# Feed-forward weights in two sets of buffers instead of one, and later due times for the fp4 weights and the softmax attention

## The chip, the cores and the metric

The kernel runs on one core of one Trainium2 chip. The metric is device time in microseconds (us) of one execution. One execution was also profiled; its trace gives every instruction's start and duration on the engines: TensorE (PE for matmuls, PEld for the loading of their stationary operand), VectorE (DVE), ScalarE (ACT), GpSimd (POOL), and the SyncE queue that issues the DMAs (SPq).

## The reference

Four blocks in a row, each added to its own input, on x of shape (8, 1024, 256), all in float32:

```python
x = x + _L0_attn_ref(_layernorm(x), ...)   # block 1: linear "flow" attention, then a GELU feed-forward
x = x + _L0_ffn_ref(_layernorm(x), ...)    # block 2: ReLU feed-forward
x = x + _L1_attn_ref(_layernorm(x), ...)   # block 3: softmax attention, one head of 256
x = x + _L1_ffn_ref(_layernorm(x), ...)    # block 4: gated feed-forward with fp4 weights
```

The parts that the change touches:

```python
# block 1, after its attention: W1 is (256, 1024), W2 is (1024, 256)
ffn = jax.nn.gelu(h @ W1 + b1, approximate=False) @ W2 + b2
return _layernorm(h + ffn, ln2_g, ln2_b)
# block 2: w1 is (256, 1024), w2 is (1024, 256)
h = jax.nn.relu(jnp.einsum('bsd,dw->bsw', x, w1) + b1)
return jnp.einsum('bsw,wd->bsd', h, w2) + b2
# block 3
scores = jnp.einsum('bqd,bkd->bqk', Q, K) / jnp.sqrt(jnp.float32(D_K))
return jnp.einsum('bqk,bkv->bqv', jax.nn.softmax(scores, axis=-1), V)
# block 4: every operand, the three weights too, is rounded to fp4 in blocks of 16 along its rows
xq = fp4_quant_dequant(x); wq = fp4_quant_dequant(w)
return jnp.einsum('bsk,nk->bsn', xq, wq)
h = jax.nn.silu(gate) * y
```

Blocks 1, 2 and 4 work on each row alone, but for the running sums along the sequence in block 1's attention; block 3 needs all 1024 rows of its sequence first.

## The kernel before

**Tiles and stages.** A chunk is 128 rows, a group is 4 chunks (512 rows), a sequence is 2 groups; there are 16 groups, p = 0 to 15. Block 1's attention (`linear_group`, `linear_span`, `linear_chunk`) runs group after group, since it carries running sums; much of it is VectorE work, and twice a group it sends a small packed tile to DRAM and reads it back spread over the partitions (`packed`, `spread`). Its result is turned into `hT`, half a group (256 rows) at a time.

**The feed-forwards** are in `dense()` (line 1300). For every group, for block 1's and block 2's weights, for each half group, there are NF = 8 steps f. A step is a first product (two matmuls, 128x256 each, `w[:, k*P:]` stationary, into a bank), an activation into a `hidden` tile on ScalarE, and, LAG = 2 steps later, a second product (`second()`, two matmuls with `hidden` stationary and `w[:, D:]` moving) that accumulates over f. In the profile each of these is four records of 128x256, in float32. So a group has 32 steps, the run 512.

**Weights.** They are read anew for every half group: `load_weights()` (line 1345) gives each step one buffer `w_ff` of [128, 512], W_FF = 5 of them in turn, and loads both halves of it together: 128 columns of W1 (two 128x128 pieces) and 128 rows of W2, 128 KB each. The buffer is held from the load until the second product of its step has been issued: the load of step n has the condition `n < W_FF + seconds[0]`, where `seconds[0]` counts second products.

**Block 4's weights** are rounded and transposed by `fp4_weights()` (line 673) in 18 pieces of at most 128x256: load into a `w_raw` tile (up to three ahead), the DVE steps of `fp4`, a square on ScalarE, two transposes on TensorE, two copies on ScalarE. The last piece sets `"fp4" in weights`, which `soft_chunk` waits for in its second half.

**Blocks 3 and 4** run in `soft_chunk(cc)` (line 1464), one for each of the 64 chunks, started by `softmax_and_fp4()` (line 1603) in order, when the whole sequence is ready (`q["normed"] == NCH`). At most 4 chunks are in work, 8 once block 1's attention is done.

**The order of the work** is made when the program is built. All parts are generators; each `yield` is a need: an engine, the tiles to wait for, banks, a condition `when`, and a due time `at`. `Plan.run` (line 290) keeps a modelled clock of each engine and of the DMA queue and takes, again and again, the need with the smallest key: the time TensorE would wait for it, then how far it is from ripe (a DMA counts as ripe 3.0 us after its buffer was last used), then other engines before TensorE, and last the due time `at`. Due times are in units of groups: block 1's attention of group p is due from p to p + 0.74, its feed-forwards from p + 1 to p + 2, the weights at p + 0.9 + n % 32 / 32. The order so found is fixed on each engine's queue and on SyncE's; on the chip an instruction that waits holds up what is behind it in its queue. Every instruction is issued through one helper, so nearly all have line 331 in the profile; they are told apart by their tiles.

Of the kernel before, what the change touches and what calls it, by code (L numbers as in the profile page):

```python
# [9 lines left out]
F32 = mybir.dt.float32  # L10
# [6 lines left out]
P = 128  # L17
D = 256
# [6 lines left out]
W_FF = 5  # L25
RES = 10
HALVES = 5
LAG = 2
# [34 lines left out]
class Plan:  # L63
# [191 lines left out]
    def pe(self, *tiles, **kw):  # L255
        return self.need("tensor", tiles, **kw)
# [7 lines left out]
    def dma(self, *tiles, **kw):  # L264
        return self.need("sync", tiles, **kw)
# [84 lines left out]
def block_stack_kernel(ctx: ExitStack, tc: tile.TileContext, a: dict, out: bass.AP):  # L350
# [20 lines left out]
    plan = Plan(tc, tc.nc)  # L371
    nc, pe, dve, act, dma = plan, plan.pe, plan.dve, plan.act, plan.dma
# [117 lines left out]
    late = set()  # L490
# [132 lines left out]
    def two(t):  # L623
        return t.rearrange("p (k t) -> p k t", k=2)
# [48 lines left out]
    def fp4_weights():  # L673
        pieces = []
        for name, dstT in (("L1_ffn_w_gate", wgT), ("L1_ffn_w_up", wuT)):
            for r0, rows in INTER_TILES:
                turns = [(dstT[:, k, r0 : r0 + rows], k * P, P) for k in range(2)]
                pieces.append((a[name][r0 : r0 + rows, :], turns))
        for n in range(2):
            for c0 in range(0, INTER, D):  # L680
                width = min(D, INTER - c0)
                turns = []
                for f0 in range(0, width, P):
                    rows = min(P, width - f0)
                    dst = wdT[:rows, (c0 + f0) // P, n * P : (n + 1) * P]
                    turns.append((dst, f0, rows))
                pieces.append((a["L1_ffn_w_down"][n * P : (n + 1) * P, c0 : c0 + width], turns))
        raws = {}
        for i, (src, turns) in enumerate(pieces):
            for j in range(i, min(i + 3, len(pieces))):  # L690
                if j not in raws:
                    ahead = pieces[j][0]
                    raws[j] = (yield from fresh(
                        "soft",
                        dma(at=1.5 + 1.6 * i / len(pieces), when=lambda: count["stage"] == 4),
                        "w_raw",
                    ))[
                        : ahead.shape[0], : ahead.shape[1]
                    ]
                    nc.sync.dma_start(out=raws[j], in_=ahead)  # L700
            rows, width = src.shape
            raw = raws.pop(i)
            at = 1.5 + 1.6 * i / len(pieces)
            yield dve(raw, at=at)
            yield from fp4(raw, width, rows)
            yield pe(raw, banks=1)
            bank = tr_bank()
            for k, (dst, c0, n) in enumerate(turns):
                nc.tensor.transpose(bank[:n, k, :rows], raw[:, c0 : c0 + n], ident[:rows, :rows])
            plan.drop(raw)  # L710
            yield act(bank)
            for k, (dst, c0, n) in enumerate(turns):
                nc.scalar.copy(dst, bank[:n, k, :rows])
        weights.add("fp4")
# [585 lines left out]
    def dense():  # L1300


        behind = []

        def second():
            p, b, half, f, hidden, w = behind.pop(0)
            acc = accs.get((p, b, half))
            yield pe(
                hidden, banks=0 if f else 1, when=None if f else lambda: count["acc"] < 2
            )  # L1310
            if f == 0:
                acc = accs[p, b, half] = mm_bank()
                plan.keep(acc)
                count["acc"] += 1

            for c in range(2):
                nc.tensor.matmul(
                    acc[:, c * D : (c + 1) * D],
                    lhsT=hidden[:, c * P : (c + 1) * P],
                    rhs=w[:, D:],  # L1320
                    start=f == 0 and c == 0,
                    stop=f == NF - 1,
                    skip_group_check=True,
                )
            plan.drop(hidden)
            seconds[0] += 1
            if f == NF - 1:
                if (b, half) == (1, 1):
                    count["dense"] += 1
                left = [2]  # L1330

                def taken():
                    left[0] -= 1
                    if not left[0]:
                        plan.let_go(acc)
                        count["acc"] -= 1

                for j in range(2):
                    norms = (norms_1, norms_2)[b]
                    plan.start(  # L1340
                        norms(p, 2 * half + j, acc[:, j * D : (j + 1) * D], taken),
                        p + 1 + (2 * b + half + 1) / 4,
                    )

        def load_weights():
            ws, n = [], 0
            for p in range(flows):
                for wa, wb in (("L0_attn_W1", "L0_attn_W2"), ("L0_ffn_w1", "L0_ffn_w2")):
                    for f in 2 * list(range(NF)):
                        yield dma(  # L1350
                            at=p + 0.9 + n % 32 / 32,
                            when=lambda: n < W_FF + seconds[0] and count["stage"] >= 2,
                            unused=ws[n - W_FF :][:1] if n >= W_FF else (),
                        )
                        w = big.tile([P, 2 * D], F32, tag="w_ff", name="w_ff", bufs=W_FF)
                        cols = slice(f * P, (f + 1) * P)
                        nc.sync.dma_start(
                            out=two(w[:, :D]), in_=a[wa][:, cols].rearrange("(k p) n -> p k n", p=P)
                        )
                        nc.sync.dma_start(out=w[:, D:], in_=a[wb][cols, :])  # L1360
                        ws.append(w)
                        loaded.append(w)
                        n += 1

        loaded, seconds = [], [0]
        plan.start(load_weights(), 0.9)
        accs = {}
        for p in range(flows):
            for b, (kind, ba, func) in enumerate((("hT", b1, AF.Gelu), ("nT", fb1, AF.Relu))):
                for half in range(2):  # L1370
                    n_turned = groups[p]["turned"]
                    while behind and n_turned.get((kind, half)) != 2:
                        yield from second()
                    for f in range(NF):
                        yield pe(
                            at=p + 1 + (16 * b + 8 * half + f) / 32,
                            when=lambda: n_turned.get((kind, half)) == 2 and loaded and "dense" in late,
                        )
                        inT = groups[p][kind][half]
                        w = loaded.pop(0)  # L1380
                        yield pe(inT, w, banks=1)
                        bank = mm_bank()[:, : 2 * P]
                        for k in range(2):
                            nc.tensor.matmul(
                                bank,
                                lhsT=w[:, k * P : (k + 1) * P],
                                rhs=inT[:, k, :],
                                start=k == 0,
                                stop=k == 1,
                            )  # L1390
                        count["stage"] = 4
                        hidden = yield from fresh("hidden", act(bank))
                        table(func)
                        nc.scalar.activation(hidden, bank, func, bias=ba[:, f : f + 1])
                        behind.append((p, b, half, f, hidden, w))
                        if f == NF - 1:
                            count["halves"] -= 1
                        if len(behind) > LAG:
                            yield from second()
        while behind:  # L1400
            yield from second()
# [62 lines left out]
    def soft_chunk(cc):  # L1464
# [1 line left out]
        g, i = divmod(c, G)  # L1466
        q = seqs[s]
        n2T, vt = q["n2T"], q["vt"]
        at = 3 + cc / 4
        yield pe(  # L1470
            banks=1,
            when=lambda: count["asked"] == cc
# [130 lines left out]
    def softmax_and_fp4():  # L1603
        for cc in range(B * NCH):
            q = seqs[cc // NCH]
            yield dve(
                at=3 + cc / 4,
                when=lambda: q["normed"] == NCH and cc - count["out"] < (8 if plan.spare else 4) and "softmax" in weights and "ends" in late,
            )
            plan.start(soft_chunk(cc), 3 + cc / 4)  # L1610

    for part in (linear_attention(), masks(), late_constants(), zeros(), load_weights_and_rows(), dense(), softmax_and_fp4(), fp4_weights(), softmax_weights()):
        plan.start(part, 0.0)
# [43 lines left out]
```

## Time and profile before

| | |
|---|---|
| median of 3 runs | 2680.63 us (2677.88 to 2684.55) |
| profiled execution, time | 2684.53 us |
| profiled execution, span from first to last instruction | 2682.8 us |
| mean granted TensorE clock | 0.988 |
| ACT busy | 1253.2 us (47%) |
| POOL busy | 585.4 us (22%) |
| mean DMA rate over the span | 79 GB/s |
| weight loads, `w_ff` | 1024 DMAs of 128 KB, median 0.46 us each on SPq |

Busy time is time in which at least one instruction of the engine runs; matmuls overlap, and the ends of their records are modelled. A clock of 0.83 in a stretch means that TensorE ran at 83% of its full speed in the mean of that stretch. The windows of the profile give the busy time of each engine in a stretch of the span; what is left of the stretch is idle time. The prediction shows the lines that it uses.

### The profile page before, as it was taken

How to read it: one execution, taken by the hardware profiler on the slowest of the kernel's cores; microseconds unless marked ns; L12 is line 12 of the kernel's file. 1: busy time of each engine (PE TensorE's matmuls, PEld its weight loads, DVE VectorE, ACT ScalarE, POOL GpSimd, SP SyncE). 2: the span in 40 equal slices, each digit the busy share in tenths (PEclk: the TensorE clock that was granted, in tenths of full speed). 3: DMA queues.
4: the chain of work that ended last, by engine and by line, in shares of the span. 5: the costliest groups of instructions: out<-in, count | busy, mean ns of one | idle time of the engine just before them, and what ended most of it. 6: DMA issues, size and time to landing. Idle time of an engine off the chain costs nothing.

```text
span 2682.8 us, 45525 instructions
## 1 busy us (share of the span) xinstructions
PE 2600.5 (97%) x16687; PEld 2020.7 (75%) x16687; DVE 1937.8 (72%) x4368; ACT 1253.2 (47%) x2600; POOL 585.4 (22%) x1101
## 2 busy tenths in 40 slices
PE   6999999999999999999999999999999999999997
PEld 4777777777777877777777777777777777787765
DVE  7788786776858768586776858668586777855565
ACT  3444445546454453544445454453545435445342
POOL 1332222131212213132221212213122221212000
PEclk8899999999999999999999999999999999999999
DMA  3334232322223232232323223132322313222000
GB/s 87 98 107 142 79 95 74 95 70 86 70 81 105 69 87 66 75 107 64 103 62 89 72 77 109 60 89 70 93 77 72 103 58 87 74 75 81 28 16 8
DMA packets 286814, 211.88 MB, mean 79 GB/s; under 512 B 24704, under 2 KB 275072, under 8 KB 286592
## 3 DMA queue, kind: packets, MB, share of 16 engines
q1 hardware_dynamic: 286592, 208.97, 26.7%
q8 instruction: 133, 2.18, 0.3%
q14 instruction: 89, 0.73, 0.1%
HBM read 188.17 MB, written 20.71 MB: 78 GB/s over the span
## 4 chain that ended last, share of the span: by engine, by line
PE 81%; DVE 12%; DMA 3%; ACT 2%; issue 1%; POOL 1%; SPq 0%; DVEq 0%; ACTq 0%; POOLq 0%
PE bank L331 81%; DVE hid L331 1%; DVE prod L331 1%; DMA spread<-packed 1%; DVE n L331 1%; ACT L331 1%; DVE ln_st L331 1%; DVE x_amax L331 1%; DVE div L331 1%; DVE res L331 1%; DVE u L331 1%; DMA packed<-scale 1%; DVE q L331 0%; DVE ln_mv L331 0%; POOL ln_rstd L331 0%
## 5 line engine op out<-in xcount | busy, mean ns | idle before, releaser
L331 PE MATMUL bank<-half,w_ff 128*128 128x256 f32 x2048 | 535.5, 384 | 15.1 <-DMA w_ff<-in_L_ffn_w_dram 7.7
L331 PE MATMUL bank<-w_ff,hidden 128*128 128x256 f32 x2048 | 532.9, 384 | 0.0
L331 POOL TENSOR_SCALAR ln_ve<-ln_mv 128x1 f32<-128x1 f32 x384 | 103.3, 269 | 1747.3 <-DVE ln_mv L331 1739.3
L331 PEld LDWEIGHTS bank<-half,w_ff 128*128 128x128 f32 x2048 | 379.8, 191 | 93.3 <-issue 24.8
L331 PEld LDWEIGHTS bank<-w_ff,hidden 128*128 128x128 f32 x2048 | 370.6, 191 | 88.5 <-issue 39.1
L331 ACT ACT_TABLE_LOAD x298 | 382.3, 1283 | 5.2
L331 ACT ACTIVATE hidden<-bank,c_L_ffn_b 128x256 f32<-128x256 f32 x256 | 120.8, 472 | 298.9 <-PE bank L331 298.9
L331 POOL TENSOR_TENSOR ln_rstd<-ln_ve,neghalf 128x1 f32<-128x1 f32 x384 | 237.5, 619 | 32.0
L331 PE MATMUL bank<-n2T,qT 128*128 128x512 f32 x512 | 242.1, 596 | 1.1 <-ACT qT L331 1.1
L331 PE MATMUL bank<-vt,probT 128*128 128x256 f32 x1024 | 232.0, 380 | 0.0
L331 PEld LDWEIGHTS bank<-vt,probT 128*128 128x128 f32 x1024 | 193.3, 190 | 32.9 <-issue 2.9
L331 ACT ACTIVATE hidden<-bank,c_L_attn_b 128x256 f32<-128x256 f32 x256 | 119.7, 468 | 193.6 <-PE bank L331 192.9
L331 DVE TENSOR_TENSOR hid<-hid,bank 128x352 f32<-128x352 f32 x118 | 60.9, 516 | 199.0 <-PE bank L331 165.4
L331 PE MATMUL bank<-wdT,hqT 128*128 128x256 f32 x768 | 177.8, 381 | 0.8 <-ACT hqT L331 0.8
L331 PE MATMUL bank<-wgT,xqT 128*128 128x352 f32 x512 | 174.9, 464 | 0.6 <-ACT xqT L331 0.5
L331 PE MATMUL bank<-wuT,xqT 128*128 128x352 f32 x512 | 172.4, 459 | 0.0
L331 DVE TENSOR_TENSOR sc<-bank,triu 128x512 f32<-128x512 f32 x256 | 160.6, 679 | 13.0 <-PE bank L331 12.0
L331 PEld LDWEIGHTS bank<-wdT,hqT 128*128 128x128 f32 x768 | 144.5, 191 | 22.9 <-issue 1.7
L331 PEld LDWEIGHTS bank<-n2T,qT 128*128 128x128 f32 x512 | 94.3, 191 | 71.7 <-issue 61.3
L331 PEld LDWEIGHTS bank<-wuT,xqT 128*128 128x128 f32 x512 | 97.5, 190 | 54.5 <-issue 0.5
L331 PEld LDWEIGHTS bank<-wgT,xqT 128*128 128x128 f32 x512 | 95.2, 191 | 36.8 <-issue 1.9
L331 PE MATMUL bank<-ident,n 128*128 128x128 f32 x512 | 93.7, 278 | 21.8 <-DVE n L331 14.5
(213 smaller groups left out, 4363.8 us busy)
## 6 DMA issues: line engine op xcount, KB each, us to landing
w_ff<-in_L_attn_W_dram SPq DMA_DIRECT2D x512, 128.0 KB
w_ff<-in_L_ffn_w_dram SPq DMA_DIRECT2D x512, 128.0 KB
spread<-packed SPq DMA_DIRECT2D x90, 256.0 KB
x<-in_L_attn_inputs_dram SPq DMA_DIRECT2D x64, 128.0 KB
xr<-in_L_attn_inputs_dram SPq DMA_DIRECT2D x64, 128.0 KB
rows<-res SPq DMA_DIRECT2D x64, 128.0 KB
out_dram<-y SPq DMA_DIRECT2D x64, 128.0 KB
rows<-rows SPq DMA_DIRECT2D x56, 128.0 KB
```

The lines of the kernel that those rows point to most:

```text
L331: ins = method(*args, **kw)
```

## The change

The first-product and the second-product weights get buffers of their own, `w_in` and `w_out`, five of [128, 256] each: the same bytes as five of [128, 512]. `load_weights` is started twice, once for each. A `w_in` buffer is taken again after the first product and the activation of its step (`firsts`), a `w_out` buffer after the second product (`seconds`). The `w_out` loads are due LAG steps later. `second()` no longer carries its weight tile along: it waits until a `w_out` has been asked for, then for its landing. The fp4 weights are due from 2.5 to 4.0 instead of 1.5 to 3.1, and every chunk of blocks 3 and 4 is due half a unit later.

```diff
@@ fp4_weights
-                        dma(at=1.5 + 1.6 * i / len(pieces), when=lambda: count["stage"] == 4),
+                        dma(at=2.5 + 1.5 * i / len(pieces), when=lambda: count["stage"] == 4),
...
-            at = 1.5 + 1.6 * i / len(pieces)
+            at = 2.5 + 1.5 * i / len(pieces)
@@ dense
         def second():
-            p, b, half, f, hidden, w = behind.pop(0)
+            p, b, half, f, hidden = behind.pop(0)
             acc = accs.get((p, b, half))
-            yield pe(
-                hidden, banks=0 if f else 1, when=None if f else lambda: count["acc"] < 2
-            )
+            yield pe(when=lambda: w_out and (f > 0 or count["acc"] < 2))
+            w = w_out.pop(0)
+            yield pe(hidden, w, banks=0 if f else 1)
...
-                    rhs=w[:, D:],
+                    rhs=w,
...
-        def load_weights():
+        def load_weights(names, used, loaded, first):
             ws, n = [], 0
             for p in range(flows):
-                for wa, wb in (("L0_attn_W1", "L0_attn_W2"), ("L0_ffn_w1", "L0_ffn_w2")):
+                for name in names:
                     for f in 2 * list(range(NF)):
                         yield dma(
-                            at=p + 0.9 + n % 32 / 32,
-                            when=lambda: n < W_FF + seconds[0] and count["stage"] >= 2,
+                            at=p + 0.9 + (n % 32 + (0 if first else LAG)) / 32,
+                            when=lambda: n < W_FF + used[0] and count["stage"] >= 2,
                             unused=ws[n - W_FF :][:1] if n >= W_FF else (),
                         )
-                        w = big.tile([P, 2 * D], F32, tag="w_ff", name="w_ff", bufs=W_FF)
+                        tag = "w_in" if first else "w_out"
+                        w = big.tile([P, D], F32, tag=tag, name=tag, bufs=W_FF)
                         cols = slice(f * P, (f + 1) * P)
-                        nc.sync.dma_start(
-                            out=two(w[:, :D]), in_=a[wa][:, cols].rearrange("(k p) n -> p k n", p=P)
-                        )
-                        nc.sync.dma_start(out=w[:, D:], in_=a[wb][cols, :])
+                        if first:
+                            nc.sync.dma_start(
+                                out=two(w), in_=a[name][:, cols].rearrange("(k p) n -> p k n", p=P)
+                            )
+                        else:
+                            nc.sync.dma_start(out=w, in_=a[name][cols, :])
...
-        loaded, seconds = [], [0]
-        plan.start(load_weights(), 0.9)
+        firsts, seconds = [0], [0]
+        w_in, w_out = [], []
+        plan.start(load_weights(("L0_attn_W1", "L0_ffn_w1"), firsts, w_in, True), 0.9)
+        plan.start(load_weights(("L0_attn_W2", "L0_ffn_w2"), seconds, w_out, False), 0.9)
...
-                            when=lambda: n_turned.get((kind, half)) == 2 and loaded and "dense" in late,
+                            when=lambda: n_turned.get((kind, half)) == 2 and w_in and "dense" in late,
...
-                        w = loaded.pop(0)
+                        w = w_in.pop(0)
...
-                        behind.append((p, b, half, f, hidden, w))
+                        firsts[0] += 1
+                        behind.append((p, b, half, f, hidden))
@@ soft_chunk
-        at = 3 + cc / 4
+        at = 3.5 + cc / 4
@@ softmax_and_fp4
-                at=3 + cc / 4,
+                at=3.5 + cc / 4,
...
-            plan.start(soft_chunk(cc), 3 + cc / 4)
+            plan.start(soft_chunk(cc), 3.5 + cc / 4)
```

## The prediction

> **What bounds the kernel now.** First the page's engine line:
>
> ```profile
> span 2682.8 us, 45525 instructions
> PE 2600.5 (97%) x16687; PEld 2020.7 (75%) x16687; DVE 1937.8 (72%) x4368; ACT 1253.2 (47%) x2600; POOL 585.4 (22%) x1101
> ```
>
> TensorE bounds it. The change removes no matmul, so it can only win TensorE's idle time, 2682.8 - 2600.5 = 82.3 us, and what a lowered clock costs. Second, the windows by stage, to see where that time lies (columns: window, its length, busy time and instructions of PE, PEld, DVE, ACT, POOL, granted clock, DMA share, GB/s):
>
> ```profile
> 0.00:75.00 75.00, 48.60 (x350) 35.71 (x350) 56.14 (x144) 22.82 (x65) 15.72 (x41) 0.81 0.31 78
> 75.00:120.00 45.00, 45.00 (x363) 35.30 (x356) 30.66 (x65) 22.45 (x49) 14.86 (x29) 0.98 0.29 82
> 120.00:140.00 20.00, 15.94 (x62) 12.24 (x60) 17.71 (x33) 4.95 (x15) 5.21 (x9) 0.83 0.66 183
> ...
> 150.00:170.00 20.00, 16.27 (x110) 12.97 (x112) 14.17 (x41) 5.73 (x16) 3.72 (x10) 0.83 0.39 116
> ...
> 230.00:250.00 20.00, 16.14 (x87) 12.32 (x86) 17.07 (x37) 5.54 (x17) 4.28 (x8) 0.83 0.62 171
> ...
> 268.00:2500.00 2232.00, 2213.63 (x14375) 1728.48 (x14372) 1612.02 (x3605) 1081.31 (x2199) 503.93 (x933) 1.00 0.28 81
> 2500.00:2546.00 46.00, 43.74 (x200) 31.71 (x199) 26.93 (x69) 16.66 (x39) 2.95 (x8) 1.00 0.07 24
> 2546.00:2613.00 67.00, 63.32 (x277) 46.40 (x276) 46.10 (x103) 30.07 (x56) 2.25 (x6) 0.97 0.06 16
> 2613.00:2682.80 69.80, 51.24 (x203) 35.18 (x201) 40.78 (x89) 18.92 (x39) 2.21 (x6) 0.93 0.02 8
> ```
>
> I count the loss of a stretch as its length minus busy time times clock. Until 75 us the feed-forwards have not begun and the change reaches nothing. From 75 to 268 us three stretches lose 20 - 15.94 x 0.83 = 6.8, 20 - 16.27 x 0.83 = 6.5 and 20 - 16.14 x 0.83 = 6.6 us; the rest there some 2. The 2232 us of the middle idle 18.4 us, under 1%. The tail after 2500 us idles 182.8 - 158.3 = 24.5 us and loses 63.32 x 0.03 + 51.24 x 0.07 = 5.5 us of clock: 30 us. So about 70 us can be touched at all.
>
> Third, TensorE's waits up to 270 us and its timeline (start, length, what, idle before it and who ended it), to see what the change can remove of this:
>
> ```profile
> PE bank L331 <- DMA w_ff<-in_L_ffn_w_dram: 6.9, 2, 3.7
> 118.48 1.03 PE L331 MATMUL bank<-half,w_ff 128*128 128x256 f32 x4
> 129.67 2.07 PE L331 MATMUL bank<-half,w_ff 128*128 128x256 f32 x4 [3.75 <-DMA w_ff<-in_L_ffn_w_dram]
> 160.10 2.11 PE L331 MATMUL bank<-qz,k 32*128 32x256 f32 x16 [3.73 <-ACT qz L331]
> 237.22 2.07 PE L331 MATMUL bank<-half,w_ff 128*128 128x256 f32 x4 [3.11 <-DMA w_ff<-in_L_ffn_w_dram]
> ```
>
> Two of the three losses are waits for feed-forward weights; the third waits for block 1's attention. After each, four matmuls that take 1.03 us take 2.07.
>
> **Edit 1, separate buffers.** Removed: nothing; added: nothing. Still 1024 loads of 128 KB and 2048 + 2048 matmul records. What moves is when a buffer comes free. In a dense stretch a step lasts 1.73 us (the first products start at 114.17, 115.03 + 0.86, and so on: 8 records in 1.73 us). Before, the buffer of step n - 5 comes free after its second product, issued LAG = 2 steps late, and is needed by the first product of step n: some 2.5 steps, 4.3 us, for the wait, the queue and the landing. In the queue at the first stall the load was issued at 124.09 us, behind four loads of the attention, and the chain of waits shows it landing 5.54 us later:
>
> ```profile
> 121.44 2.55 SPq L331 DMA_DIRECT2D spread<-packed  x4
> 124.09 1.04 SPq L331 DMA_DIRECT2D w_ff<-in_L_ffn_w_dram  x2
> 124.09 5.54 DMA w_ff<-in_L_ffn_w_dram
> ```
>
> After, either kind has the five steps from its own use to its next, 8.65 us, 4.3 more than before. The two stalls idled 3.75 and 3.11 us, so both are covered. Gain: at most 6.8 + 6.6 = 13.4 us, at least 0, if TensorE merely meets the next wait earlier. I take 11: the 20 us stretches also hold waits for transposes of 0.65 and 0.75 us that stay, and the lead is only half a microsecond above the first stall.
>
> The Trainium skill, "TensorE: Matmul & The Clock Gate", section Part 1, has the clock fall to half only after an idle window of about 3.4 us; by that the 3.11 us wait would cost its own length alone, and this term would be nearer 9 than 11. The trace disagrees: after 3.11 us the four matmuls still took 2.07 us, and the clock of the stretch was 0.83; the measurement decides.
>
> Edit 1's costs: a pair of loads that had one need has two, so SyncE may stop at 512 more places. SPq issues take a median of 0.46 us, 1024 x 0.46 = 471 us of 2683, hidden under the matmuls; queued behind a load that waits are the `x`, `xr`, `rows`, `packed` and `spread` transfers. First-weight loads now wait for an earlier event, second-weight loads for the same as before, so I cost it at 0. If the cover is gone, a late `spread` is what the third stall shows: 6.5 us. The new first yield of `second()` waits for nothing on the chip: 0.
>
> **Edit 2, fp4 weights due later.** Nothing is removed. 18 pieces move as a whole: 18 DMAs, 36 transposes (PE 7.5 us), 18 squares and the copies on ACT, and on DVE the 90 instructions on `w_raw`, 40.35 us, plus three small ones a piece: 18 x (0.198 + 0.252 + 0.251) = 12.6, together 53 us.
>
> ```profile
> 70.00:268.00 198.00, 5.46 (x26) 3.39 (x26) 29.93 (x67) 5.85 (x14) 0.93 0.41 118
> 268.00:402.00 134.00, 132.35 (x1029) 102.82 (x1028) 108.25 (x249) 64.84 (x141) 35.10 (x68) 1.00 0.30 87
> 402.00:536.00 134.00, 130.64 (x783) 100.15 (x773) 95.69 (x207) 70.55 (x142) 23.50 (x47) 1.00 0.29 84
> ```
>
> The first line is `w_raw` alone: 29.93 of the 40.35 us, so 39 of the 53, fall before 268 us, where DVE is the crowded engine (17.71 of 20 us at the first stall). They give way to block 1's attention. About a third lies before 160 us ((4.14 + 5.41)/40.35 x 53 = 12.5 us by the windows of 70 to 160 us), and that is what the third stall's chain can come earlier: enough for its 6.5 us and for the 6 us by which edit 1 brings TensorE there sooner. Gain 0 to 8.8 (the third stall and the 2 us of rest); I take 4, since part of the chain is DMA round trips (3.2 us of the wait) that DVE does not shorten. Cost: the 39 us land between 268 and 536 us, where DVE has 268 - 108.25 - 95.69 = 64 us free. They fit, but raise it to 0.9. A stall such as the ramp's costs 6.5 us; 0 to 2 of them, 0 to 13 us; I take 2.
>
> **Edit 3, attention due half a unit later.** A unit is 128 second-product records; 1678 in the 2100 us from 300 to 2400 make it 160 us, so 80 us, or two chunks of 40, later. Where both are ready, the next groups' linear attention and feed-forwards now go first, and the chunks stay as filler for TensorE's waits. The middle has 18.4 us of idle to win and could as well gain some: -9 to +9, both half of that; I take -1.5. No row shows the new order. The tail: ten outputs are written after the last feed-forward step at 2500 us; two more would make twelve, and the step ends earlier by their matmuls, 2 x 15.8 us (158.3/10). Priced at the tail's rate before its last 70 us, (2.3 + 3.7 + 1.9)/113 = 7%, two chunks lose 2.2 us; at the rate of the last 70 us, (69.8 - 51.24 x 0.93)/69.8 = 32%, 10 us; a gain of 3 is the bound below, if they fill waits of the last groups. The drain of the last chunks itself is there in either kernel, so the first rate is nearest: +2.
>
> **The sum.** -11 - 4 + 2 - 1.5 + 2 = -12.5 us. On the profiled execution, a span of 2682.8 and 1.7 around it, 2684.5 us, this gives 2672.0. That execution lies 3.9 above the median shown, 2680.6, so the median becomes 2668 us (-0.47%).
>
> **The rivals.** *The stall moves on, no change (0.27).* TensorE's lead in the ramp is lost at the next wait for block 1's attention, whose chain is round trips through DRAM rather than DVE's throughput. For it: the stall at 160 us ends on the chain DVE q, itself 3.2 us behind a spread transfer. Against it: DVE was busy 88% at the weight stalls. Of the 12.5 only some 3 to 6 remain: 2676 us.
>
> *The crowd moves, slower (0.18).* The fp4 pieces meet the start of the softmax chunks between 268 and 536 us and DVE becomes the bound there: two stalls of 6.5, 13 us, and the last two chunks drain at 32% loss, 10 us, against 11 + 4 won: -15 + 23 = +8, and with an even middle 2689 us. It decides from the point where DVE's share in 268 to 536 us goes above the 0.88 at which the ramp stalled. For it: 204 + 39 = 243 us of 268 is 0.91. Against it: the pieces come last among ready needs, and there are attention chunks to fill TensorE, as there were not in the ramp.
>
> *The buffers do nothing.* If the plan goes on placing the loads late (it takes a load as ripe 3.0 us after the last use), the lead is 4.3 us in name only, and the two weight waits stay: 2668 + 11 = 2679. I count it with the second case of no change.
>
> **How the numbers follow.** The forecast has 0.55, its own range -22 to -8.5 us, 2659 to 2672. A measurement of this kernel can tell about 0.3%, 8 us, from no change. Faster than 2672.6: 0.56; within: 0.27; slower than 2688.7: 0.17. With all bounds won (13.4 + 8.8 + 9) it would be 2650; I take that as the low end, and the slower rival's 2689 as the high end.
>
> **What would show it.** Right: no wait of TensorE for `w_in` or `w_out` over 1 us; the stretches of 120 to 140 and 230 to 250 us busy over 19 with a clock over 0.95; `w_raw` work mostly after 268 us; the last feed-forward step some 30 to 45 us before 2500; eleven or twelve outputs behind it. Wrong: DVE waits of TensorE over 3 us between 268 and 536 us, idle in the middle well above 18 us, a tail that loses over 36 us, or weight waits that stay.

## The result: 0.2% slower

The changed kernel takes 2688.23 us in the median of 8 runs (2685.74 to 2690.88), the kernel before, run beside it, 2683.01 (2677.88 to 2687.43). The ratio is 1.002, with a 95% interval of 1.001 to 1.0029: slower by about 5 us, where 12.5 us of gain had been forecast. The profiled execution took 2688.08 us, with a span of 2686.4, 3.6 more than before's.

The changed kernel's page and its windows by stage (columns as in the prediction):

```profile
span 2686.4 us, 46037 instructions
PE 2597.6 (97%) x16687; PEld 2015.4 (75%) x16687; DVE 1949.5 (73%) x4368; ACT 1283.1 (48%) x2628; POOL 560.5 (21%) x1101
```

```profile
75.00:120.00 45.00, 45.00 (x362) 35.85 (x361) 31.52 (x68) 22.51 (x52) 15.64 (x29) 1.00 0.36 102
120.00:140.00 20.00, 16.96 (x107) 13.51 (x106) 18.12 (x36) 7.08 (x17) 4.32 (x9) 1.00 0.69 198
...
150.00:170.00 20.00, 17.85 (x226) 14.37 (x227) 15.85 (x38) 6.85 (x18) 5.45 (x12) 0.91 0.24 71
...
230.00:250.00 20.00, 18.45 (x115) 14.75 (x114) 18.95 (x52) 7.33 (x20) 8.39 (x16) 1.00 0.47 138
```

```profile
268.00:2500.00 2232.00, 2198.05 (x14160) 1711.34 (x14159) 1615.32 (x3593) 1095.11 (x2214) 476.15 (x924) 1.00 0.28 80
2500.00:2686.40 186.40, 165.14 (x708) 119.46 (x706) 122.34 (x276) 80.77 (x149) 6.64 (x18) 0.95 0.04 13
```

By the prediction's count the three bad stretches of the ramp now lose 3.0, 3.8 and 1.6 us instead of 6.8, 6.5 and 6.6. The middle, from 268 to 2500 us, idles 34.0 us instead of 18.4. The gain is there, and it is lost again.

Who ended TensorE's waits, first in the ramp (75 to 268 us), then in the middle (who waited for whom, us in total, times, longest), of the changed kernel:

```profile
PE bank L331 <- DVE n L331: 2.6, 3, 2.2
PE bank L331 <- ACT e L331: 1.8, 2, 1.4
PE bank L331 <- DVE w_raw L331: 1.2, 1, 1.2
```

```profile
PE bank L331 <- DVE sc L331: 7.5, 8, 1.7
PE bank L331 <- DVE v L331: 5.3, 9, 1.4
PE bank L331 <- DVE res L331: 3.6, 3, 1.2
PE bank L331 <- DVE kv L331: 3.3, 3, 1.1
PE bank L331 <- DVE prod L331: 3.1, 3, 1.4
```

No matmul waits for a feed-forward weight any more. In the middle the kernel before had one group of any size, 9.2 us for `v`:

```profile
PE bank L331 <- DVE v L331: 9.2, 12, 1.7
PE bank L331 <- ACT prob L331: 3.0, 6, 0.9
PE bank L331 <- issue: 1.4, 1, 1.4
```

Now there are a dozen small ones, and their counts of 3 are the trail. TensorE's timeline has one of them at 856.9, 1506.0 and 2154.3 us:

```profile
856.92 1.13 PE L331 MATMUL bank<-wo,xo 128*128 128x256 f32 x4 [1.72 <-DVE sc L331]
...
1506.00 1.13 PE L331 MATMUL bank<-wo,xo 128*128 128x256 f32 x4 [1.73 <-DVE sc L331]
...
2154.30 1.13 PE L331 MATMUL bank<-wo,xo 128*128 128x256 f32 x4 [1.72 <-DVE sc L331]
```

The distance is 649.1 and 648.3 us, the wait the same to 10 ns. **The plan has settled into a cycle**, here of two sequences, and every miss in it comes back each time round. Before's cycle was one sequence long. Its one large wait stands in its timeline 321 us apart:

```profile
1186.06 0.44 PE L331 MATMUL bank<-ident,n 128*128 128x128 f32 x2 [1.25 <-DVE v L331]
...
1506.81 0.44 PE L331 MATMUL bank<-ident,n 128*128 128x128 f32 x2 [1.72 <-DVE v L331]
...
1827.98 0.44 PE L331 MATMUL bank<-ident,n 128*128 128x128 f32 x2 [1.09 <-DVE v L331]
```

So I split the span by work done instead of by the clock: at the start of the last second-product matmul of each sequence's feed-forwards (read from the traces). "Chunks out" counts the output rows finished by then.

```
us                      before   changed   difference of the step
end of sequence 1        292.0     275.3    -16.7
end of sequence 2        607.8     562.4    -28.7
end of sequence 7       2213.7    2183.9    +15.6   (five sequences: 321.2 and 324.3 each)
end of sequence 8       2500.8    2472.4     +1.4
end of the span         2682.8    2686.4    +32.0
chunks out at 2, 8       6, 54     4, 52
sum                                          +3.6
```

Most of the -28.7 and of the +32.0 are the same two chunks, put off at the beginning and done at the end. What decides is 16.7 us won at first and 15.6 us lost, 3.1 us in each of five sequences. The loss is idle time of TensorE. In sequences 3 to 7 it idles 1605.90 - 1594.68 = 11.2 us before and 25.8 us changed, 14.6 more, at the full clock:

```profile
607.80:2213.70 1605.90, 1594.68 (x10364) 1243.60 (x10363) 1168.06 (x2604) 778.05 (x1582) 369.01 (x673) 1.00 0.28 81
562.40:2183.90 1621.50, 1595.73 (x10356) 1240.80 (x10355) 1185.75 (x2607) 800.37 (x1606) 350.42 (x675) 1.00 0.28 80
```

The first line is the kernel before, the second the changed one. The end of a sequence is a mark in the feed-forwards alone, and other work can lie on either side of it. At the end of sequence 1 the changed kernel has started 1928 matmul records and the kernel before 1946; by the usual spacing of the 18 that differ, an estimate, some 2.6 of the 16.7 us are work put off, and some 14 are won.

### The profile page after: what moved, and what is told of

Its sections match the earlier page's. It is cut to its first block, busy times and chain, and to the rows that moved or that the text cites. A ratio compares the mean times of both kernels' runs of the same rounds, so it can differ in the third digit from the quotient of the medians.

```text
span 2686.4 us, 46037 instructions
## 1 busy us (share of the span) xinstructions
PE 2597.6 (97%) x16687; PEld 2015.4 (75%) x16687; DVE 1949.5 (73%) x4368; ACT 1283.1 (48%) x2628; POOL 560.5 (21%) x1101
## 4 chain that ended last, share of the span: by engine, by line
PE 64%; DVE 26%; ACT 4%; DMA 3%; issue 2%; POOL 1%; SPq 0%; DVEq 0%; POOLq 0%; ACTq 0%
PE bank L331 64%; DVE hid L331 4%; DVE prod L331 4%; DVE n L331 2%; DVE ln_st L331 2%; DMA spread<-packed 2%; DVE u L331 1%; ACT L331 1%; DVE x_amax L331 1%; DVE res L331 1%; DVE spread L331 1%; DVE div L331 1%; DVE ln_mv L331 1%; DMA packed<-flow 1%; DVE x_r L331 1%
## 5 line engine op out<-in xcount | busy, mean ns | idle before, releaser
L331 PE MATMUL bank<-half,w_in 128*128 128x256 f32 x2048 | 529.7, 381 | 7.1 <-DVE kv L331 3.3
L331 PE MATMUL bank<-w_out,hidden 128*128 128x256 f32 x2048 | 532.1, 383 | 0.0
L331 POOL TENSOR_SCALAR ln_ve<-ln_mv 128x1 f32<-128x1 f32 x384 | 96.5, 251 | 1799.2 <-DVE ln_mv L331 1763.9
L331 PEld LDWEIGHTS bank<-w_out,hidden 128*128 128x128 f32 x2048 | 369.7, 190 | 94.7 <-issue 42.9
L331 PEld LDWEIGHTS bank<-half,w_in 128*128 128x128 f32 x2048 | 377.8, 190 | 79.7 <-issue 20.5
L331 POOL TENSOR_TENSOR ln_rstd<-ln_ve,neghalf 128x1 f32<-128x1 f32 x384 | 228.9, 596 | 32.0
```

The lines of the kernel that those rows point to most:

```text
L331: ins = method(*args, **kw)
```

## The experiments

Theory A: the buffers win in the ramp, and the later attention leaves linear attention uncovered in the middle, the more the later. Theory B: the buffers themselves lose in the middle. Theory C: any new order falls into some cycle, and which one is not ordered by the size of the edit. Each run was timed beside the kernel before on the same chip; the last columns are from its one profiled execution, as in the table above. "Each" is an average over five sequences. It is the length of a cycle where these agree, which from sequence 4 on they mostly do to within 3 us; in `after_4` they take 316 to 330 us, in `after_late_15` 328 to 335 and in `after_late_30` 310 to 348, and there it is an average and no more.

```
run             ratio   95% interval     seq 1   seqs 3-7, each   after seq 8   span
before                                   292.0   321.2           182.0         2682.8
changed         1.0020  1.0010-1.0029    275.3   324.3           214.0         2686.4
buffers_alone   0.9991  0.9982-1.0000    297.2   320.1           181.6         2681.7
attn_alone      1.0012  1.0003-1.0021    290.1   322.7           207.5         2685.5
fp4_alone       1.0035  1.0022-1.0048    297.7   321.5           182.0         2691.4
due_alone       1.0032  1.0021-1.0042    296.1   322.1           207.0         2688.8
after_325       1.0005  0.9996-1.0014    276.3   323.5           194.9         2684.0
after_4         1.0030  1.0017-1.0042    278.9   322.0           246.6         2691.4
after_ripe20    1.0004  0.9994-1.0015    292.3   321.4           204.7         2681.3
before_ripe20   1.0102  1.0088-1.0116    297.8   324.2           185.2         2705.7
buffers_fp4mid  0.9989  0.9980-0.9997    280.9   320.1           183.1         2676.7
buffers_attn    1.0002  0.9993-1.0011    297.5   321.9           208.9         2684.5
after_ripe_late 0.9949  0.9935-0.9962    276.6   320.4           211.7         2667.1
attn_275        1.0156  1.0142-1.0170    291.3   325.7           178.8         2723.1
after_late_15   1.0155  1.0141-1.0169    275.5   331.2           215.9         2727.3
after_late_30   0.9983  0.9975-0.9992    275.0   324.6           204.7         2675.0
fp4mid_late_20  1.0038  1.0025-1.0052    282.1   324.5           179.6         2694.6
before_late_20  1.0087  1.0073-1.0100    291.9   324.1           185.1         2705.2
```

**One edit at a time.** `buffers_alone` is the changed kernel with the due times of before; the other three are the kernel before with one or both due times of the change.

```diff
# buffers_alone, from the changed kernel
-            at = 2.5 + 1.5 * i / len(pieces)
+            at = 1.5 + 1.6 * i / len(pieces)
...
-        at = 3.5 + cc / 4
+        at = 3 + cc / 4
# attn_alone, from the kernel before
-        at = 3 + cc / 4
+        at = 3.5 + cc / 4
# fp4_alone, from the kernel before
-            at = 1.5 + 1.6 * i / len(pieces)
+            at = 2.5 + 1.5 * i / len(pieces)
# due_alone, from the kernel before: both of these
```

> Separate weight buffers, all due times as before. Theory A (the buffers win in the ramp, the later attention loses in the middle): 10 to 15 us faster than before, the stretch from 75 to 268 us loses 9 to 12 us instead of 22, the middle from 268 to 2500 us idles 18 to 22 us as before. Theory B (the buffers themselves lose in the middle, since feed-forward steps now run in one go and no longer cover the linear attention): within 5 us of before, the ramp wins its 10 us, the middle idles about 30 us. Theory C (any new order of the plan scatters the middle by some 10 us): no telling.

> One set of weight buffers as before, fp4 weights due as before, softmax attention due half a unit later. Theory A: 10 to 15 us slower than before, with 30 us or more of idle in the middle, the two weight waits of the ramp still there. Theory B: within 4 us of before, the middle at 18 to 22 us. Theory C: the middle anywhere from 15 to 35 us.

> One set of weight buffers as before, attention due as before, fp4 weights due from 2.5 to 4.0. All theories: the 6.5 us wait for block 1's attention at 160 us goes or halves, 2 to 6 us won there; some of it may be lost between 268 and 536 us, where the first attention chunks then wait for the weights. Within 6 us of before; a middle after 536 us that idles over 25 us would speak for theory C.

> One set of weight buffers as before, both due times later. Theory A: 5 to 12 us slower than before, the middle idles 30 us or more. Theory B: 0 to 5 us faster, the middle at 18 to 22 us. Theory C: the middle anywhere from 15 to 35 us, not the sum of the two single edits.

Only `due_alone` lands in theory A's range, 0.32% slower, and not by its reason: its middle idles 25.8 us. The buffers alone win next to nothing, and sequence 1 even ends 5.2 us later than before. Part of that is other work done sooner (2026 matmul records started, not 1946); at the end of sequence 3, where both kernels have started 6118, it is 1.7 us behind. The ramp's waits of `buffers_alone` say why:

```profile
PE bank L331 <- DVE n L331: 4.8, 4, 1.7
PE bank L331 <- DVE scale L331: 3.6, 1, 3.6
PE bank L331 <- DVE w_raw L331: 2.7, 2, 1.4
PE bank L331 <- DMA w_in<-in_L_ffn_w_dram: 2.3, 1, 2.3
PE bank L331 <- ACT qz L331: 1.9, 1, 1.9
PE bank L331 <- DMA w_out<-in_L_ffn_w_dram: 1.3, 1, 1.3
```

The weight waits fall from 6.9 to 3.6 us, and TensorE, ahead of VectorE now, stands still for `n`, `scale` and `w_raw` instead: the stall has moved on. The fp4 weights put off alone lose as well: sequence 1 ends at 297.7 us, and at the end of sequence 2, with 4036 records started in both kernels, it is 7.2 us behind. One weight wait of 3.5 us stays, a new wait of 4.9 us for `w_raw` comes, and the wait near 160 us, which all theories had expected to go or halve, is there with 3.99 us, on `n`. It came out 0.35% slower, some 9.5 us, outside the 6 us of all theories. Theory B falls: with the buffers alone the middle idles 17.4 us, 320.1 us a sequence. The attention put off makes the cycle longer, 322.7, but the whole comes to 3 us slower, where theory A asked for 10 to 15.

**The size of the shift, and the margin.** `after_325` and `after_4` are the changed kernel with the attention due at 3.25 and 4. Nearly all waits of the middle are under 1.75 us. Theory D therefore: they are matmuls that the plan takes too early, by its own clock, while other work stands ready; then a larger margin of ripeness, 2.0 us for TensorE instead of 1.0, removes them.

```diff
# after_ripe20, before_ripe20
-    RIPE = {"tensor": 1.0, "vector": 0.5, "scalar": 0.5, "gpsimd": 0.0, "sync": 3.0}
+    RIPE = {"tensor": 2.0, "vector": 0.5, "scalar": 0.5, "gpsimd": 0.0, "sync": 3.0}
```

> The changed kernel with the attention due at 3.25 instead of 3.5. The middle of each kernel is a cycle of the plan that repeats once a sequence (320.6 us before) or once in two (648.7 us changed, 324.4 a sequence), and the same waits of 0.4 to 1.7 us come back in each. Theory A (the later the attention, the less covers the linear attention): a cycle between, 322 to 323 us a sequence, 4 to 8 us faster than the changed kernel. Theory C (any other order gives another cycle with other waits, not ordered by the shift): a cycle anywhere from 320 to 326 us.

> The changed kernel with the attention due at 4.0. Theory A: more of the same, 326 us or more a sequence, 8 us or more slower than the changed kernel less 2 to 4 us won in the tail. Theory C: a cycle anywhere from 320 to 326 us, faster or slower than the changed kernel.

> The changed kernel with TensorE work counted as ripe 2.0 us after its inputs by the plan's clock, not 1.0. The waits of the middle are nearly all under 1.75 us. Theory D (they are places where the plan's clock runs about a microsecond ahead of VectorE, and other work stood ready): the waits in the middle fall from 33 us of idle to under 12, a cycle of 321 us or less a sequence, 12 to 20 us faster than the changed kernel. Theory A: they stay, as nothing else is there to cover; within 5 us of the changed kernel.

> The kernel before with the same 2.0 us. Theory D: the middle's idle falls from 18 us to under 8, 5 to 10 us faster than before. Theory A and C: within 5 us of before.

The shift does not order the cycles: 323.5, 324.3 and 322.0 us at 3.25, 3.5 and 4, against theory A, which asked for 326 or more at 4. The margin shortens the changed kernel's cycle to 321.4, the way that theory D points but not as far (the middle idles 20.7 us, not under 12), and it takes back the ramp's gain (292.3). That in the ramp nothing else stands ready is the likely reason; it was not tested. On the kernel before it does the contrary of theory D: 1.0% slower.

**Which two of the three, and both gains at once.** `buffers_fp4mid` is the changed kernel with the attention due at 3 and the fp4 weights from 2.0; `buffers_attn` has the fp4 weights as before. `after_ripe_late` sets the margin only after the ramp. `attn_275` is the kernel before with the attention due earlier.

```diff
# after_ripe_late, from the changed kernel, at the end of fp4_weights
         weights.add("fp4")
+        plan.RIPE = {**plan.RIPE, "tensor": 2.0}
```

> Separate buffers, fp4 weights due from 2.0 to 3.5, attention due at 3 as before: the changed kernel without its attention edit (with fp4 due at 2.5 and the attention at 3 the plan finds no order). If the later attention is what makes the cycle of the plan longer: 320 to 321 us a sequence, the first sequence's feed-forwards done 5 to 17 us earlier than before, 5 to 15 us faster than before. If the two other edits do it: 323 us or more a sequence, and not faster.

> Separate buffers, fp4 weights due as before, attention due at 3.5. If the first stage's gain needs the buffers and the later fp4 weights together: no gain in the ramp, a cycle of 322.5 to 324.5 us a sequence, 5 to 12 us slower than before. If the attention's edit alone frees the ramp: the first sequence's feed-forwards done 10 us or more earlier.

> The changed kernel, TensorE work ripe 1.0 us after its inputs until the last fp4 weight piece is placed, 2.0 us after that. If the ramp's gain and the short cycle can be had together: the ramp as in the changed kernel (first sequence's feed-forwards done near 275 us), a cycle of 320 to 321 us a sequence, 10 to 16 us faster than before. If the cycle is a matter of chance: anywhere from 320 to 326 us a sequence, 16 us faster to 12 us slower.

> The kernel before with the attention due at 2.75, earlier than before. If later attention means less cover and earlier more: a cycle of 320 us or less a sequence, with fewer waits in the middle than before's 18 us, less some 3 us for a tail with one chunk fewer: 0 to 5 us faster than before. If 3 is merely a due time at which the plan falls into a good cycle: 322 us or more, 5 us or more slower.

This settles what the ramp's gain needs: separate buffers and later fp4 weights together. Sequence 1 ends between 275.0 and 282.1 us in all seven other kernels with both and the margin of 1.0 in the ramp; with one of them or none, and in the two with 2.0 throughout, between 290.1 and 297.8. `buffers_attn`, without the fp4 edit, has none of the gain, as forecast, but its 321.9 us a sequence is shorter than the 322.5 to 324.5 expected, and it is as fast as before.

`buffers_fp4mid` meets its expectation only in part. It has the short cycle, 320.1, and ends sequence 1 11.1 us earlier, but it is 0.11% faster, some 3 us, where 5 to 15 were expected: at the end of sequence 3, with 6118 records started in both kernels, it is 4.6 us ahead of before. With the attention due at 3 (and the fp4 weights from 2.0) less than half of the gain lasts.

`after_ripe_late` keeps that start and has a short cycle, 320.4 us: 0.51% faster than before, the fastest of all. Its windows:

```profile
75.00:268.00 193.00, 185.01 (x1440) 147.87 (x1436) 153.61 (x354) 84.39 (x202) 61.80 (x119) 0.99 0.45 126
268.00:2500.00 2232.00, 2215.64 (x14298) 1727.68 (x14287) 1622.31 (x3628) 1100.90 (x2242) 486.27 (x927) 1.00 0.28 80
```

The middle idles 16.4 us, the changed kernel's 34.0. And `attn_275` ends theory A for good: with the attention due earlier the cycle is longer still, 325.7.

**Is it the margin, or luck?** Two more margins after the ramp, 1.5 and 3.0, and 2.0 on the two kernels with the attention due at 3.

```diff
# after_late_15, after_late_30, from the changed kernel
         weights.add("fp4")
+        plan.RIPE = {**plan.RIPE, "tensor": 1.5}   # 3.0 in after_late_30
# fp4mid_late_20 from buffers_fp4mid, before_late_20 from the kernel before
+        plan.RIPE = {**plan.RIPE, "tensor": 2.0}
```

> The changed kernel, TensorE work ripe after 1.5 us instead of 1.0 once the fp4 weights are placed (with 2.0 it was 0.51% faster than before, cycle 320.7 us a sequence). If the changed cycle's waits are work taken about a microsecond early, with other work standing ready (theory D): between, 321 to 323 us a sequence, 4 to 12 us faster than before. If each setting draws its cycle by chance (theory C): anywhere from 320 to 326, the two sides of 2.0 unlike it.

> The same with 3.0 us. Theory D: 320 to 321.5 us a sequence, 10 to 16 us faster than before, since waits over 1.75 us were hardly there to remove. Theory C: anywhere from 320 to 326 us.

> Separate buffers, fp4 weights due from 2.0, attention due at 3, ripe after 2.0 us from the fp4 weights on. Theory D: the cycle falls from 320.1 to 319 us or so, 4 to 10 us faster than before. Theory C: like the kernel before with 2.0 throughout (325.4), 15 us slower or more, or anything between.

> The kernel before, ripe after 2.0 us from the fp4 weights on (2.0 throughout was 1.0% slower, 325.4 us a sequence at the end). If the attention due at 3 and the margin of 2.0 do not go together: again near 325 us a sequence, 15 to 25 us slower than before. If that was the cycle which the ramp led into: another cycle, 320 to 323.

Not the margin alone. A margin of 1.0 gives 324.3 us a sequence, 1.5 gives 331.2, 2.0 gives 320.4 and 3.0 gives 324.6 in the mean, and nobody could have told which beforehand. In `after_late_15`, between two better ones, the middle's waits are longer, and they too come back each time round:

```profile
PE bank L331 <- DVE res L331: 12.3, 6, 2.2
PE bank L331 <- DVE kv L331: 11.5, 10, 1.6
PE bank L331 <- ACT prob L331: 9.9, 11, 1.6
```

```profile
1023.86 1.13 PE L331 MATMUL bank<-half,w_in 128*128 128x256 f32 x4 [2.16 <-DVE res L331]
...
1353.95 1.13 PE L331 MATMUL bank<-half,w_in 128*128 128x256 f32 x4 [2.16 <-DVE res L331]
...
1683.53 1.13 PE L331 MATMUL bank<-half,w_in 128*128 128x256 f32 x4 [2.16 <-DVE res L331]
```

Theory D falls as a rule. What is left is theory C: the averages lie between 320.1 and 331.2 us, and neither due time nor margin alone orders them. Two regularities remain.

Due time and margin act as a pair. At the margin of 1.0 the four kernels with the attention due at 3 have 320.1 to 321.5, the six with it later 321.9 to 324.3, the one earlier 325.7. At 2.0, throughout or after the ramp, it is the other way round: the three with the attention due at 3 have 324.1 to 324.5, the two at 3.5 320.4 and 321.4. `before_late_20` answers its own question too: its last sequences take 325.4 us as those of `before_ripe20` do, though its sequence 1 ends 6 us earlier, so there it is not the ramp that decides.

The attention's edit moved the kernel out of a good cycle, but it is not the whole of the 3.1 us. In the three pairs at the margin of 1.0 that differ in this edit alone it costs 1.5 (before and `attn_alone`), 1.8 (`buffers_alone` and `buffers_attn`) and 0.6 us a sequence (`fp4_alone` and `due_alone`). From `buffers_attn` to the changed kernel only the fp4 edit is new, and the average goes from 321.9 to 324.3. Yet its last matmul on `w_raw` starts at 397.6 us, in sequence 2; in the middle nothing is left of this edit but the order into which it led the plan.

Why 3 is a good place at 1.0, and whether it would be in another kernel, stays open; so does where the plan's clock first departs from the chip's, which was not tried.

## Why the prediction was wrong

- **Edits 1 and 2 in the ramp: -11 - 4 + 2 = -13, near as a sum, wrong as terms.** Sequence 1 ends 16.7 us earlier. Up to the end of sequence 2 the changed kernel (562.4) and `attn_alone` (575.4) have the same attention edit and all but the same number of matmul records started (3906 and 3910), and the other two are worth -13.0. That this meets the sum is partly luck: with the attention due at 3 the two are worth only 4.6 us (`buffers_fp4mid`, fp4 weights from 2.0). And neither wins alone: where as many records have been started as before, the buffers are 1.7 us behind and the fp4 weights 7.2. The 11 took both weight waits as covered; with the buffers alone 3.6 us of them stay. The text had the reason, that edit 2 brings the chain forward by about what edit 1 brings TensorE forward, and then priced the two separately. The first rival, the stall that moves on, is what the buffers do alone.
- **What the fp4 weights cost later: 2, not settled.** Between the ends of sequences 1 and 2, `buffers_fp4mid` takes 325.2 us and `buffers_alone` 315.5, 9.7 more, inside the bounds of 0 to 13. But in that step it also starts 2118 matmul records, not 2022, by their usual spacing some 5 us of work (an estimate), so only the rest can be a cost. And less moved than was assumed: of the 29.93 us of DVE work on `w_raw` that lay before 268 us the prediction let all go, and 21.58 stayed. The changed kernel's windows for `w_raw` alone (window, length, then PE, PEld, DVE, ACT, clock, DMA share, GB/s):

```profile
70.00:268.00 198.00, 3.42 (x18) 2.28 (x18) 21.58 (x50) 4.14 (x10) 0.98 0.43 123
268.00:536.00 268.00, 3.56 (x18) 2.09 (x18) 18.56 (x40) 3.21 (x8) 1.00 0.33 93
```

- **The attention put off, in the tail: +2, near in the changed kernel.** Two chunks more were left, as forecast (twelve, the last step 28.4 us earlier). `attn_alone` shows what they are worth: 32.4 us won by the end of sequence 2, 1.9 of them in sequence 1. The changed kernel's tail is 32.0 us longer, a net of -0.4. But the tail of `attn_alone` itself is only 25.5 us longer, so there the term is a gain of some 5 us, beyond the bound of 3.
- **The middle: "-9 to +9, both half of that; I take -1.5". This is the step that failed.** Measured +15.6 us in sequences 3 to 7, outside the bounds, and a middle that idles 34.0 us, one of the prediction's own signs of being wrong. It was taken as scatter to both sides around the order of before, with no row for the new one. But the plan repeats its order, so what a new order loses counts once for each cycle, and there was little to win: the kernel before idles 18.4 us in the whole middle. How much there was to lose, no row of before could show; the runs did. Of 17 other kernels only three have a lower average than its 321.2 us a sequence, the best 320.1; the others are higher by up to 10.0. A term that leans to the slow side, and with it a forecast near no change, is what they support.
- **The slower rival** put the loss where the fp4 weights meet the first chunks. Some of that crowding may exist (part of the 9.7 us above), but it was paid out of the ramp's gain; the loss that made the kernel slower came after it. That the rival's 2689 us lies so near the measured 2688.2 is luck. The separate loads themselves cost nothing that shows: 512 more instructions on the page, and in the middle of `buffers_alone` no matmul waits for a weight, at 320.1 us a sequence.

## What to carry to other kernels

Where an order is planned once and repeats, look for the period first: a wait of a microsecond that comes back each cycle is worth its number of repetitions, and a kernel whose cycle is already 99% full may have little to win and more to lose by any edit that makes the plan choose anew: 14 of 17 variants here had a longer average. Do not price two edits separately when one moves the waiting engine and the other what it waits for; here neither won alone, and both together won some 14 us in the first sequence. When two kernels are compared at a mark, count the work done by then. And when a plan's settings are changed, try several, because neighbours can lie 3% apart in the time of a sequence.

## What the runs showed of the hardware

A wait of some 2 us can be followed by half the clock. After 2.19 us of idle at 152 us in the changed kernel, sixteen 32-row matmuls took 2.11 us, the same form 8 us later 1.17:

```profile
152.15 1.09 PE L331 MATMUL bank<-ident,n 128*128 128x128 f32 x4 [2.19 <-DVE n L331]
153.17 2.11 PE L331 MATMUL bank<-qz,k 32*128 32x256 f32 x16
...
161.65 1.17 PE L331 MATMUL bank<-qz,k 32*128 32x256 f32 x16
```

The granted clock of 150 to 160 us was 0.83. In `after_late_15` 2.16 us at 1023.86 us cost nothing: four matmuls in 1.13 us. So the idle time alone does not decide. (The prediction counts such a row of the kernel before, 2.11 us at 160.10 us, among "four matmuls that take 1.03 us"; it was sixteen of 32 rows, the form that takes 1.17 here.) The Trainium skill, "TensorE: Matmul & The Clock Gate", section Part 1, gives a free-running window of about 3.4 us and lets the clock fall after at least one idle window. Both waits are shorter than that, and the first was followed by the slow clock all the same.

Busy time is no measure of TensorE's work to a few microseconds. Idle rose by 6.5 us (82.3 to 88.8) and the lowered clock cost 6.8 less, yet the span rose by 3.6, with the same 16687 matmuls. The records of 379 ns overlap, four of them in 1.03 us, so the first 0.16 us of a wait can hide in the record before it; the changed kernel has 80 waits over 0.15 us and the kernel before 65, which makes some 2.4 us of the difference (an estimate) and leaves the rest open. The Trainium skill, "Perfetto Trace Analysis", section Identifying the Most-Contended Engine, says that matmul busy time is no good measure of how close a kernel is to roofline. No run here measures that distance; what this case shows is that busy time also misjudges a difference of a few microseconds between two kernels with the same matmuls, and it is why the span above is split at marks of the work.
